# An LSTM layer with a residual: another order of the hidden units, row-wise weight copies, and x and the output moved in runs of 128 bytes

## The chip, the cores and the metric

The kernel runs on one core of a Trainium2 chip. The metric is the device time of one execution in microseconds. Before the change it was 2294.73 us (median of 3 runs, 2294.44 to 2298.69).

## The reference

x has shape (16, 512, 512): 16 sequences of 512 time steps with 512 features. `h0` (called `cond_1024`) is (16, 512), `Wx` and `Wh` are (512, 2048), `b` is (2048). All are float32.

```python
xW = einsum('ntd,dg->ntg', x, Wx) + b
def step((prev_h, prev_c), xw_t):
    a = xw_t + prev_h @ Wh
    i, f, o = sigmoid(a[:, :512]), sigmoid(a[:, 512:1024]), sigmoid(a[:, 1024:1536])
    g = tanh(a[:, 1536:])
    next_c = f * prev_c + i * g
    next_h = o * tanh(next_c)
return x + (next_h of all 512 steps)
```

The 512 steps depend on each other; `xW` does not depend on them, and can be computed ahead of the step that needs it.

## The kernel before

**Units and partitions.** There are 128 partitions, cut into four blocks of 32 (`NJ` = 4, index j). Each block takes 128 of the 512 hidden units or input features. With feature = 128j + 32c + u, partition block j holds the features 128j to 128j+127, of which the 32 x 32 transposes of VectorE bring feature u of chunk c to partition 32j + u. The rows of `Wx` and `Wh` have to lie in the same order: chunk c of partition 32j + u is row 128j + 32c + u. `load_w` (L124) copies a weight in transfers that each fill 32 partitions, two chunks at a time; its copies of `Wh` are issued by SP and ACT (4 each, L341), those of `Wx` by SP and POOL (8 each, L359).

**Steps and stages.** A stage is 8 time steps (`XB`), so there are 64 stages. Two steps form a pair, since 16 sequences fill half of a 32-row block; a stage has 4 pairs (`XP`). `load_xs` (L141) loads the x of one stage into a tile `xs` of 128 x 4 x 128: for each of the 4 feature blocks and each of the 2 steps of a pair it issues one DMA on SP's queue, of 16 partitions x 4 pairs x 512 bytes. That is 8 DMAs per stage. Stage s+2 is loaded in the first step of stage s (L519); `xs` has four buffers (L77).

**A step on the engines.** The program's order on each engine is written out by hand: `STEP_PE` and `STEP` name the operations of one step, and the loop from L485 emits them. TensorE runs `products` (L182, matmul at L188): the hidden state, in three float16 parts, times three float16 parts of `Wh` (`wq`), 96 matmuls of 256 columns per step, in groups of four that write the four 32-row blocks of a bank. Then `project` (L163, matmul at L165) computes `xW` of a later pair: 16 float32 matmuls of 512 columns per step. VectorE and ScalarE turn the gates into the next hidden state. In odd steps `turn_x` (L158) transposes the x of a later pair, of pair (t+5)/2 in step t, so the first pair of stage s is turned in step 8s-5. In even steps `residual` (L320) transposes the finished pair on VectorE and adds x on POOL into a tile `ob` (two buffers, L79).

**Output.** After the fourth pair of a stage `put` (L311) writes the whole `ob` with 8 DMAs on SP's queue, of 16 partitions x 4 pairs x 512 bytes. For the last two pairs it is called earlier, so that little is left at the end. In SP's queue the put of stage s-1 stands directly ahead of the load of stage s+2.

**DMA semaphores.** The DMAs of the SP and ACT queues go round over eight semaphores, and each DMA waits until the one that used its semaphore last has landed. At most eight are under way.

**The start.** Before step 0 the kernel finds the largest magnitude of each half of `Wh` (`bound`, L394), derives scales, splits `Wh` into its three float16 parts (`split`, L426) in 8 rounds n, turns x and h0 (L469, in round 3), projects the first two pairs (round 4), seeds the gate banks (`seed`, L174), and then runs step 0 with `first_products` (L197). The bias arrives by 8 broadcast DMAs on POOL's queue.

Of the kernel before, what the change touches and what calls it, by code (L numbers as in the profile page):

```python
# [7 lines left out]
FP = mybir.dt.float32  # L8
HP = mybir.dt.float16
I32 = mybir.dt.int32  # L10
AF = mybir.ActivationFunctionType
ALU = mybir.AluOpType
# [3 lines left out]
Q = 32  # L16
# [13 lines left out]

@with_exitstack
def lstm_residual(ctx: ExitStack, tc: tile.TileContext, x, h0, wx, wh, b, out):

# [61 lines left out]
    wh_sb = const.tile([P, NK, G * H], FP, tag="wh", name="wh_sb")  # L97
    wq = [const.tile([P, NK, G * H], HP, tag=f"wq{i}", name=f"wq{i}") for i in range(3)]

    wx_j = wx_sb.rearrange("p c (g j w) -> p c j g w", g=G, j=NJ)  # L100
    wh_j = wh_sb.rearrange("p c (e g j h u) -> p c e h j g u", e=2, g=2, j=NJ, h=2)
    wq_j = [w.rearrange("p c (g j h u) -> p c h j g u", g=G, j=NJ, h=2) for w in wq]
    bias = const.tile([P, G * P], FP, tag="bias", name="bias")
    mask = const.tile([P, S2], FP, tag="mask", name="mask")
    zero = const.tile([1, G * P], HP, tag="zero", name="zero")
    amax = const.tile([P, NK], FP, tag="amax", name="amax")
    top = const.tile([P, 2], FP, tag="top", name="top")
    bits = const.tile([P, 2, 2], FP, tag="bits", name="bits")
    sc = const.tile([P, 2, 4], FP, tag="sc", name="sc")
# [11 lines left out]
    ]  # L121
    xb = [psum.tile([P, G * P], FP, tag=f"xb{i}", name=f"xb{i}") for i in range(NXB)]

    def load_w(dst, w, c0, dmas, parts=1):  # L124


        n = G * H // parts
        for j in range(2):
            for q, dma in enumerate(dmas):
                r = w[(2 * q + j) * P + c0 * Q :][: 2 * Q].rearrange("(c u) f -> u c f", u=Q)  # L130
                p = slice((2 * q + j) * Q, (2 * q + j + 1) * Q)
                for e in range(parts):
                    a = parts - 1 - e
                    dma.dma_start(  # L134
                        out=dst[p, c0 : c0 + 2, a * n : (a + 1) * n],
                        in_=r[:, :, e * n : (e + 1) * n],
                    )

    xs = {}

    def load_xs(s, dma=nc.sync):  # L141

        xs[s] = xsp.tile([P, XP, P], FP, tag="xs", name=f"xs_{s}")
        for j in range(NJ):
            for r in range(S2):
                p0 = j * Q + r * N
                dma.dma_start(
                    out=xs[s][p0 : p0 + N],
                    in_=x[:, s * XB + r : (s + 1) * XB : S2, j * P : (j + 1) * P],
                )  # L150


    xT = {}
# [3 lines left out]

    def turn_x(q):  # L158
        s, i = divmod(q, XP)
        xT[q] = xtp.tile([P, NK, Q], FP, tag="xT", name=f"xT_{q}")  # L160
        nc.vector.transpose(xT[q].rearrange("p c m -> p (c m)"), xs[s][:, i])

    def project(q, c):  # L163
        for j in range(NJ):
            nc.tensor.matmul(  # L165
                xb[q % NXB][j * Q : (j + 1) * Q],
                lhsT=xT[q][:, c],
                rhs=wx_j[:, c, j],
                start=False,
                stop=(c == NK - 1),  # L170
                skip_group_check=True,
            )

# [135 lines left out]
        nc.scalar.mul(hs[p][:, a], hist[p // XP][:, p % XP, a], RSL[h])  # L309

    def put(s, i0, i1, dmas):  # L311
        for j in range(NJ):
            for r in range(S2):
                p0 = j * Q + r * N
                dmas[r % len(dmas)].dma_start(
                    out=out[:, s * XB + S2 * i0 + r : s * XB + S2 * i1 : S2, j * P : (j + 1) * P],
                    in_=ob[s][p0 : p0 + N, i0:i1],
                )

    def residual(p):  # L320
        s, i = divmod(p, XP)
        if i == 0:
            ob[s] = outp.tile([P, XP, P], FP, tag="ob", name=f"ob_{s}")
        hb = work.tile([P, P], FP, tag="hb", name=f"hb_{p}")
        nc.vector.transpose(hb, hs[p].rearrange("p c m -> p (c m)"))  # L325
        nc.gpsimd.tensor_tensor(ob[s][:, i], hb, xs[s][:, i], ALU.add)  # L326
        if p == NP - 1:
            put(s, i, i + 1, [nc.sync, nc.scalar])
        elif p == NP - 2:
            put(s, 0, i + 1, [nc.sync])  # L330
        elif i == XP - 1:
            put(s, 0, XP, [nc.sync])


    h_in = work.tile([P, P], FP, tag="h_in", name="h_in", bufs=1)
# [1 line left out]
    warm = const.tile([1, 1], FP, tag="warm", name="warm")  # L337
    brow = const.tile([1, G * H], FP, tag="brow", name="brow")
    ones = const.tile([1, Q], FP, tag="ones", name="ones")
    for c in (0, 2):  # L340
        load_w(wh_sb, wh, c, (nc.sync, nc.scalar))  # L341
    load_xs(0)
    nc.vector.memset(zero, 0.0)
    nc.vector.memset(h_in, 0.0)
    nc.vector.memset(ones, 1.0)
    for j in range(NJ):
        nc.sync.dma_start(out=h_in[j * Q : j * Q + N], in_=h0[:, j * P : (j + 1) * P])
    nc.gpsimd.dma_start(out=brow, in_=b.rearrange("(o f) -> o f", o=1))
    b_j = b.rearrange("(o e g j w) -> j e o g w", o=1, e=2, g=2, j=NJ)
    for j in range(NJ):  # L350
        for e in range(2):
            nc.gpsimd.dma_start(
                out=bias[j * Q : (j + 1) * Q, (1 - e) * GU : (2 - e) * GU].rearrange(
                    "p (g w) -> p g w", g=2
                ),
                in_=b_j[j, e].broadcast_to([Q, 2, P]),
            )
    for c in (0, 2):
        load_w(wx_sb, wx, c, (nc.sync, nc.gpsimd), 2)  # L359
    load_xs(1)  # L360

    for h in range(2):
# [14 lines left out]

    for bank in gates[0] + gates[1] + xb[3:]:  # L380
        zeros(bank, True)
    for bank in xb[:3]:
        for e in range(2):
            for j in range(NJ):
                nc.tensor.matmul(
                    bank[j * Q : (j + 1) * Q, (1 - e) * GU : (2 - e) * GU],
                    lhsT=ones,
                    rhs=brow.rearrange("p (e g j w) -> p e j g w", e=2, g=2, j=NJ)[:, e, j],
                    start=(e == 0),
                    stop=False,  # L390
                    skip_group_check=True,
                )

    def bound(c):  # L394
        if c == 1:
            junk = tmp.tile([P, G * H], HP, tag="junk", name="junk", bufs=1)
            nc.scalar.activation(junk, wh_sb[:, c], AF.Abs, accum_out=amax[:, c : c + 1])
        else:
            nc.vector.tensor_reduce(
                amax[:, c : c + 1],  # L400
                wh_sb[:, c],
                mybir.AxisListType.X,
                ALU.max,
                apply_absolute_value=True,
            )

    def scales(h):


        nc.vector.tensor_tensor(  # L410
            top[:, h : h + 1], amax[:, 2 * h : 2 * h + 1], amax[:, 2 * h + 1 : 2 * h + 2], ALU.max
        )
        t = top[:, h : h + 1].bitcast(I32)
        e, inv = bits[:, h, 0:1], bits[:, h, 1:2]
        nc.vector.tensor_scalar(
            inv.bitcast(I32), t, EXP, EXP, ALU.bitwise_and, ALU.bitwise_xor
        )
        nc.vector.tensor_scalar(e.bitcast(I32), t, EXP, None, ALU.bitwise_and)
        nc.vector.tensor_scalar(RS2[h], inv, 2.0**12, 0.5, ALU.mult, ALU.min)
        nc.vector.tensor_scalar(RS[h], inv, 2.0**13, 1.0, ALU.mult, ALU.min)  # L420
        nc.vector.tensor_scalar(S[h], e, 2.0**-14, 1.0, ALU.mult, ALU.max)
        nc.vector.tensor_scalar(RSL[h], RS[h], 1.0 / LO, None, ALU.mult)
# [3 lines left out]
    def split(n, k):  # L426

        c, e = divmod(n, 2)
        w = wh_sb[:, c, e * GH : (e + 1) * GH]
        f = [q[:, c, (1 - e) * GH : (2 - e) * GH] for q in wq]  # L430
        if k == 0:
            nc.scalar.mul(f[0], w, RS2[c // 2])
        elif k == 1:
            r1[n] = tmp.tile([P, GH], FP, tag="r1", name=f"r1_{n}")
            nc.vector.scalar_tensor_tensor(
                r1[n], w, RS[c // 2], f[0], ALU.mult, ALU.subtract
            )
        elif k == 2:
            nc.scalar.copy(f[1], r1[n])
        elif k == 3:  # L440
            r2[n] = tmp.tile([P, GH], FP, tag="r2", name=f"r2_{n}")
            nc.vector.tensor_tensor(r2[n], r1[n], f[1], ALU.subtract)
        else:
            nc.scalar.mul(f[2], r2[n], LO)

    NH = 2 * NK
    bound(0)
    bound(1)
    scales(0)
    split(0, 0)  # L450
    split(0, 1)
    split(1, 0)
    for n in range(NH):
        if n == 0:
            bound(2)
        if n == 2:
            bound(3)
            scales(1)
        if n + 1 < NH:
            split(n + 1, 1)  # L460
# [6 lines left out]
        if n == 3:  # L467
            for q in range(3):
                turn_x(q)  # L469
            nc.vector.transpose(hT0.rearrange("p c m -> p (c m)"), h_in)  # L470
        if n == 4:
            for c in range(NK):
                for q in range(2):
                    project(q, c)

            for _ in range(16):
                zeros(xb[3], False)
        if n == 6:
            for h in range(2):
                seed(0, h)  # L480
    split(NH - 1, 4)
    for h in range(2):
        seed(1, h)

    for t in range(T):  # L485
        s, ti = divmod(t, XB)
# [22 lines left out]
            if q + 1 < NP:  # L509
                turn_x(q + 1)  # L510
        else:
            if q + 1 < NP:
                put_bias(q + 1)
            if t:
                residual(t // 2 - 1)
# [33 lines left out]
```

## Time and profile before

| what | value |
|---|---|
| median of 3 runs | 2294.73 us |
| the profiled execution: time / span | 2294.09 us / 2291.7 us |
| granted clock of TensorE | 0.999 |
| PE busy | 2249.4 us, 98% |
| DVE, ACT, POOL busy | 1952.7 us (85%), 1838.1 us (80%), 127.2 us (6%) |
| SP: DMAs issued for x and for the output | 512 and 516 |
| first matmul of step 0 | 50.87 us after the start |

The span runs from the first to the last instruction. Busy time does not count instructions that issue DMAs, so SP has no row in the page's first part; its issues are seen in the timeline of its queue, where each piece has a start, a length and a count. In the list of waits a line says who waited for whom, how long in total and how often.

### The profile page before, as it was taken

The page shows a single profiled execution, that of the slowest core. Times are in us where ns is not written, and L with a number is a line of the kernel's source. Part 1 is how long each engine was busy: PE and PEld are TensorE (multiplying, and loading weights), DVE is VectorE, ACT ScalarE, POOL GpSimd, SP SyncE. Part 2 cuts the span into 40 slices and gives each one's busy share as a digit, 9 for nine tenths or more (in the row PEclk, how much of TensorE's full clock was granted, in tenths as well). Part 3 has the DMA queues.
Part 4 walks back from the last instruction along what each step waited for, and adds up shares of the span by engine and source line. Part 5 has one row for each costly group of instructions (what it writes and reads, how often), then busy time and mean ns, then how long its engine had stood idle before and what let it go on. Part 6 is the DMA issues. An engine that isn't in the chain of part 4 may idle for free.

```text
span 2291.7 us, 137735 instructions
## 1 busy us (share of the span) xinstructions
PE 2249.4 (98%) x57445; PEld 1572.7 (69%) x57445; DVE 1952.7 (85%) x11813; ACT 1838.1 (80%) x7959; POOL 127.2 (6%) x281
## 2 busy tenths in 40 slices
PE   4999999999999999999999999999999999999997
PEld 2677766777766777777666777776677777666775
DVE  5888888888888888888888888888888888888887
ACT  5888888888888888888888888888888888888887
POOL 1000000000000000000000000000000000000000
PEclk9999999999999999999999999999999999999999
DMA  7000000100100001000001001010000010010000
GB/s 166 13 21 15 22 18 17 22 15 20 22 14 22 22 13 22 21 14 22 17 18 22 15 20 22 13 22 22 13 22 19 17 22 18 17 22 15 20 18 12
DMA packets 85005, 51.10 MB, mean 22 GB/s; under 512 B 17104, under 2 KB 82720, under 8 KB 83872
## 3 DMA queue, kind: packets, MB, share of 16 engines
q1 hardware_dynamic: 83008, 37.82, 7.6%
q8 instruction: 452, 7.41, 1.4%
q0 software_dynamic: 928, 2.37, 0.5%
q10 hardware_dynamic: 448, 2.13, 0.4%
q14 instruction: 169, 1.38, 0.2%
HBM read 25.47 MB, written 16.78 MB: 18 GB/s over the span
## 4 chain that ended last, share of the span: by engine, by line
PE 98%; DMA 2%; DVE 0%; issue 0%; ACTq 0%; POOLq 0%; POOL 0%; SPq 0%
PE gates L188 59%; PE xb L165 38%; DMA wh_sb<-in_L_cond_Wh_dram 1%; DMA xs<-in_x_dram 0%; DMA wx_sb<-in_L_cond_Wx_dram 0%; PE gates L201 0%; PE xb L374 0%; ACTq L134 0%; DVE gt L224 0%; DVE preo L231 0%; DVE pre L231 0%; DVE parts L284 0%; DVE gto L224 0%; POOLq L544 0%; POOL ob L326 0%
## 5 line engine op out<-in xcount | busy, mean ns | idle before, releaser
L188 PEld LDWEIGHTS <-parts 128*32 128x32 f16 x49056 | 1307.1, 96 | 368.8 <-DVE parts L284 298.8
L188 PE MATMUL gates<-wq,parts 128*32 128x256 f16 x49056 | 1449.2, 273 | 4.2 <-DVE parts L284 4.2
L165 PE MATMUL xb<-wx_sb,xT 128*32 128x512 f32 x8192 | 977.1, 593 | 22.5 <-DMA wx_sb<-in_L_cond_Wx_dram 22.5
L224 DVE STREAM_TRANSPOSE gt<-gates 128x192 f32<-128x192 f32 x1024 | 391.7, 383 | 229.9 <-PE gates L188 170.7
L165 PEld LDWEIGHTS xb<-wx_sb,xT 128*32 128x32 f32 x8192 | 264.6, 110 | 327.5 <-issue 303.5
L258 ACT ACTIVATE gc<-pre 128x32 f32<-128x32 f32 x1022 | 234.7, 230 | 274.7 <-DVE pre L231 261.9
L175 ACT ACTIVATE gates<-xb,mask 128x256 f32<-128x256 f32 x1024 | 450.3, 440 | 2.1 <-PE xb L165 2.1
L266 ACT ACTIVATE os<-so,sc 128x32 f32<-128x32 f32 x1024 | 329.1, 321 | 16.6
L288 ACT COPY parts<-parts 128x32 f16<-128x32 f16 x1022 | 214.4, 210 | 131.7 <-DVE parts L284 131.7
L231 DVE SCALAR_TENSOR_TENSOR pre<-gt 128x96 f32<-128x96 f32 x1024 | 253.6, 248 | 0.0
L260 ACT ACTIVATE sif<-pre 128x64 f32<-128x64 f32 x1024 | 245.7, 240 | 0.0
L326 POOL TENSOR_TENSOR ob<-hb,xs 128x128 f32<-128x128 f32 x256 | 117.1, 457 | 2146.0 <-DVE hb L325 1732.5
L224 DVE STREAM_TRANSPOSE gto<-gates 128x64 f32<-128x64 f32 x1024 | 229.6, 224 | 0.0
L276 ACT ACTIVATE tch<-gc 128x32 f32<-128x32 f32 x1024 | 226.8, 221 | 0.3
L298 DVE SCALAR_TENSOR_TENSOR parts<-rem,parts 128x32 f16<-128x32 f32 x1022 | 196.3, 192 | 35.5
L264 ACT ACTIVATE so<-preo 128x32 f32<-128x32 f32 x1024 | 226.4, 221 | 0.0
L231 DVE SCALAR_TENSOR_TENSOR preo<-gto 128x32 f32<-128x32 f32 x1024 | 192.6, 188 | 17.5
L290 DVE SCALAR_TENSOR_TENSOR parts<-parts,hist 128x32 f16<-128x32 f16 x1022 | 192.0, 188 | 17.7
L268 DVE TENSOR_TENSOR pr<-sif,gc 128x64 f32<-128x64 f32 x1022 | 204.2, 200 | 0.0
L284 DVE TENSOR_TENSOR parts<-os,tch 128x32 f16<-128x32 f32 x1022 | 196.5, 192 | 0.0
L274 DVE TENSOR_TENSOR gc<-pr 128x32 f32<-128x32 f32 x1024 | 192.1, 188 | 0.0
L278 DVE SCALAR_TENSOR_TENSOR hist<-os,tch 128x32 f32<-128x32 f32 x1024 | 188.7, 184 | 0.3 <-ACT tch L276 0.3
(47 smaller groups left out, 730.8 us busy)
## 6 DMA issues: line engine op xcount, KB each, us to landing
xs<-in_x_dram SPq DMA_DIRECT2D x512, 32.0 KB, 2.0
out_dram<-ob SPq DMA_DIRECT2D x504, 32.0 KB, 1.7
wh_sb<-in_L_cond_Wh_dram ACTq DMA_DIRECT2D x4, 512.0 KB, 13.4
wh_sb<-in_L_cond_Wh_dram SPq DMA_DIRECT2D x4, 512.0 KB, 13.1
wx_sb<-in_L_cond_Wx_dram POOLq DMA_DIRECT2D x8, 256.0 KB, 9.5
wx_sb<-in_L_cond_Wx_dram SPq DMA_DIRECT2D x8, 256.0 KB, 6.8
bias<-in_L_cond_b_dram POOLq DMA_DIRECT2D x8, 32.0 KB, 13.4
out_dram<-ob SPq DMA_DIRECT2D x8, 24.0 KB, 1.6
```

Of the source, the lines that this page charges most:

```text
L165: nc.tensor.matmul(xb[q % NXB][j * Q : (j + 1) * Q], lhsT=xT[q][:, c], rhs=wx_j[:, c, j], start=False, stop=(c == NK - 1), skip_group_chec ...
L175: nc.scalar.mul(gates[h][t % 2][:, :GU].rearrange("p (g u) -> p g u", g=G), xb[t // 2 % NXB].rearrange("p (g h u) -> p h g u", g=G, h=2)[: ...
L188: nc.tensor.matmul(g[j * Q : (j + 1) * Q, :GU], lhsT=a[:, cc, k * N : (k + 2) * N], rhs=wq_j[i - 1][:, 2 * kh + cc, h, j], start=False, st ...
L224: nc.vector.transpose(gt.rearrange("p b m -> p (b m)"), gates[h][t % 2][:, b0 * Q : b1 * Q])
L231: nc.vector.scalar_tensor_tensor(pre.rearrange("p g (c n) -> p (g c) n", c=2), gt[:, :, (1 - t % 2) * N : (2 - t % 2) * N], 1.0 / LO, gt[: ...
L258: nc.scalar.activation(gc[h][:, 0], v["pre", h][:, 0], AF.Tanh)
L260: nc.scalar.activation(new("sif", t, h, [P, 2, 2 * N]), v["pre", h][:, 1:3], AF.Sigmoid)
L264: nc.scalar.activation(new("so", t, h, [P, 2 * N]), v["preo", h][:, 0], AF.Sigmoid)
L266: nc.scalar.mul(new("os", t, h, [P, 2 * N]), v["so", h], S[h])
L268: nc.vector.tensor_tensor(new("pr", t, h, [P, 2, 2 * N]), v["sif", h], gc[h], ALU.mult)
L276: nc.scalar.activation(new("tch", t, h, [P, 2 * N]), gc[h][:, 1], AF.Tanh)
L288: nc.scalar.copy(slots(t, h, 2), slots(t, h, 0))
```

## The change

**Other order of the units.** Feature 128c + 32j + u now lies on partition 32j + u of chunk c, for the inputs, the hidden state and the gates. Chunk c of a weight is then 128 consecutive rows, one for each partition. Each weight is copied by 8 DMAs of 128 partitions x 1024 columns (4 KB rows), all on SP's queue; ACT and POOL no longer copy weights. Block j of x and of the output is now four runs of 32 floats (128 bytes) for each time step, 128 floats apart, in place of one run of 512 bytes.

**x and output.** A DMA [...] covers one time step: `load_xs` issues 32 DMAs of 8 KB per stage, in place of 8 of 32 KB. `put` likewise, and it is called for each pair (8 DMAs of 8 KB) in place of each stage. The x of stage 0 goes over POOL's queue. Ahead of the first transpose of a stage VectorE copies one column of each pair into a small tile `seen`, which waits for all DMAs of the stage at once.

**Matmul operands.** The column order of the gates in PSUM is g, c, u. The moving operands are views of the weights: `wq` in runs of 32 float16 (64 bytes, before 128), `wx_sb` in runs of 32 float32 (128 bytes, before 512).

**Start.** The bias no longer comes by 8 DMAs; ScalarE copies it once from a bank that TensorE has filled. `brow` is loaded over ACT's queue. The bound of the last chunk of `Wh` is shared between ScalarE and VectorE, two of the eight last parts of the split go to VectorE, the projections come one round earlier, 12 in place of 16 filling matmuls with zeros follow them (into a gate bank), and the seeds of both first steps come together.

```diff
-    wx_j = wx_sb.rearrange("p c (g j w) -> p c j g w", g=G, j=NJ)
-    wq_j = [w.rearrange("p c (g j h u) -> p c h j g u", g=G, j=NJ, h=2) for w in wq]
+    wx_j = wx_sb.rearrange("p k (g c j u) -> p k j g c u", g=G, c=NK, j=NJ)
+    wq_j = [
+        w.rearrange("p k (g h c j u) -> p k h j g c u", g=G, h=2, c=2, j=NJ) for w in wq
+    ]
...
+    x_j = x.rearrange("n t (c j u) -> j n t c u", c=NK, j=NJ)
+    out_j = out.rearrange("n t (c j u) -> j n t c u", c=NK, j=NJ)
...
     def load_xs(s, dma=nc.sync):
         xs[s] = xsp.tile([P, XP, P], FP, tag="xs", name=f"xs_{s}")
-        for j in range(NJ):
-            for r in range(S2):
-                p0 = j * Q + r * N
-                dma.dma_start(
-                    out=xs[s][p0 : p0 + N],
-                    in_=x[:, s * XB + r : (s + 1) * XB : S2, j * P : (j + 1) * P],
-                )
+        for i in range(XP):
+            for j in range(NJ):
+                for r in range(S2):
+                    p0 = j * Q + r * N
+                    dma.dma_start(
+                        out=xs[s][p0 : p0 + N, i].rearrange("p (c u) -> p c u", c=NK),
+                        in_=x_j[j, :, s * XB + i * S2 + r],
+                    )
...
     def turn_x(q):
         s, i = divmod(q, XP)
+        if i == 0:
+            seen = tmp.tile([P, XP], FP, tag="seen", name=f"seen_{s}")
+            nc.vector.tensor_copy(seen, xs[s][:, :, 0])
...
     def put(s, i0, i1, dmas):
-        for j in range(NJ):
-            for r in range(S2):
-                p0 = j * Q + r * N
-                dmas[r % len(dmas)].dma_start(
-                    out=out[:, s * XB + S2 * i0 + r : s * XB + S2 * i1 : S2, j * P : (j + 1) * P],
-                    in_=ob[s][p0 : p0 + N, i0:i1],
-                )
+        for i in range(i0, i1):
+            for j in range(NJ):
+                for r in range(S2):
+                    p0 = j * Q + r * N
+                    dmas[r % len(dmas)].dma_start(
+                        out=out_j[j, :, s * XB + S2 * i + r],
+                        in_=ob[s][p0 : p0 + N, i].rearrange("p (c u) -> p c u", c=NK),
+                    )
...
         if p == NP - 1:
             put(s, i, i + 1, [nc.sync, nc.scalar])
-        elif p == NP - 2:
-            put(s, 0, i + 1, [nc.sync])
-        elif i == XP - 1:
-            put(s, 0, XP, [nc.sync])
+        else:
+            put(s, i, i + 1, [nc.sync])
...
-    for c in (0, 2):
-        load_w(wh_sb, wh, c, (nc.sync, nc.scalar))
-    load_xs(0)
+    nc.scalar.dma_start(out=brow, in_=b.rearrange("(o f) -> o f", o=1))
+    for c in range(NK):
+        for e in range(2):
+            f = slice(e * GH, (e + 1) * GH)
+            nc.sync.dma_start(out=wh_sb[:, c, f], in_=wh[c * P : (c + 1) * P, f])
+    load_xs(0, nc.gpsimd)
...
-    for c in (0, 2):
-        load_w(wx_sb, wx, c, (nc.sync, nc.gpsimd), 2)
+    for c in range(NK):
+        for e in range(2):
+            nc.sync.dma_start(
+                out=wx_sb[:, c, (1 - e) * GH : (2 - e) * GH],
+                in_=wx[c * P : (c + 1) * P, e * GH : (e + 1) * GH],
+            )
     load_xs(1)
```

More of the change, by code (lines that the diff above doesn't have):

```diff
@@ L98, in lstm_residual @@
     wq = [const.tile([P, NK, G * H], HP, tag=f"wq{i}", name=f"wq{i}") for i in range(3)]
-    wx_j = wx_sb.rearrange("p c (g j w) -> p c j g w", g=G, j=NJ)
-    wh_j = wh_sb.rearrange("p c (e g j h u) -> p c e h j g u", e=2, g=2, j=NJ, h=2)
-    wq_j = [w.rearrange("p c (g j h u) -> p c h j g u", g=G, j=NJ, h=2) for w in wq]
+    wx_j = wx_sb.rearrange("p k (g c j u) -> p k j g c u", g=G, c=NK, j=NJ)
+    wh_j = wh_sb.rearrange(
+        "p k (e g h c j u) -> p k e h j g c u", e=2, g=2, h=2, c=2, j=NJ
+    )
+    wq_j = [
+        w.rearrange("p k (g h c j u) -> p k h j g c u", g=G, h=2, c=2, j=NJ) for w in wq
+    ]
     bias = const.tile([P, G * P], FP, tag="bias", name="bias")
@@ L105, in lstm_residual @@
     zero = const.tile([1, G * P], HP, tag="zero", name="zero")
-    amax = const.tile([P, NK], FP, tag="amax", name="amax")
+    amax = const.tile([P, NK + 1], FP, tag="amax", name="amax")
     top = const.tile([P, 2], FP, tag="top", name="top")
@@ L122, in lstm_residual @@
     xb = [psum.tile([P, G * P], FP, tag=f"xb{i}", name=f"xb{i}") for i in range(NXB)]
[L124 to L133, printed above, removed]
-                    dma.dma_start(
-                        out=dst[p, c0 : c0 + 2, a * n : (a + 1) * n],
-                        in_=r[:, :, e * n : (e + 1) * n],
-                    )
+    x_j = x.rearrange("n t (c j u) -> j n t c u", c=NK, j=NJ)
+    out_j = out.rearrange("n t (c j u) -> j n t c u", c=NK, j=NJ)
+    h0_j = h0.rearrange("n (c j u) -> j n c u", c=NK, j=NJ)
     xs = {}
@@ L143, in load_xs @@
         xs[s] = xsp.tile([P, XP, P], FP, tag="xs", name=f"xs_{s}")
-        for j in range(NJ):
-            for r in range(S2):
-                p0 = j * Q + r * N
-                dma.dma_start(
-                    out=xs[s][p0 : p0 + N],
-                    in_=x[:, s * XB + r : (s + 1) * XB : S2, j * P : (j + 1) * P],
-                )
+        for i in range(XP):
[6 more added lines that the diff above has]
+                    )
     xT = {}
@@ L169, in project @@
                 start=False,
-                stop=(c == NK - 1),
+                stop=False,
                 skip_group_check=True,
@@ L311, in put @@
     def put(s, i0, i1, dmas):
-        for j in range(NJ):
-            for r in range(S2):
-                p0 = j * Q + r * N
-                dmas[r % len(dmas)].dma_start(
-                    out=out[:, s * XB + S2 * i0 + r : s * XB + S2 * i1 : S2, j * P : (j + 1) * P],
-                    in_=ob[s][p0 : p0 + N, i0:i1],
-                )
+        for i in range(i0, i1):
[6 more added lines that the diff above has]
+                    )
     def residual(p):
@@ L345, in lstm_residual @@
     nc.vector.memset(ones, 1.0)
+    load_xs(0, nc.gpsimd)
     for j in range(NJ):
[L347 to L350, printed above, removed]
+        nc.sync.dma_start(
+            out=h_in[j * Q : j * Q + N].rearrange("p (c u) -> p c u", c=NK), in_=h0_j[j]
+        )
+    for c in range(NK):
         for e in range(2):
[L352 to L356, printed above, removed]
-            )
-    for c in (0, 2):
-        load_w(wx_sb, wx, c, (nc.sync, nc.gpsimd), 2)
+            nc.sync.dma_start(
+                out=wx_sb[:, c, (1 - e) * GH : (2 - e) * GH],
+                in_=wx[c * P : (c + 1) * P, e * GH : (e + 1) * GH],
+            )
     load_xs(1)
@@ L376, in zeros @@
         )
-    for bank in gates[0] + gates[1] + xb[3:]:
+    for bank in gates[0] + gates[1]:
         zeros(bank, True)
-    for bank in xb[:3]:
+    for bank in xb:
         for e in range(2):
@@ L387, in lstm_residual @@
                     lhsT=ones,
-                    rhs=brow.rearrange("p (e g j w) -> p e j g w", e=2, g=2, j=NJ)[:, e, j],
+                    rhs=brow.rearrange("p (e g c j u) -> p e j g c u", e=2, g=2, c=NK, j=NJ)[
+                        :, e, j
+                    ],
                     start=(e == 0),
@@ L392, in lstm_residual, with bound @@
                 )
[L394 to L397, printed above, removed]
+    nc.scalar.copy(bias, xb[0])
+    def bound(i, c, on_act, f=slice(0, G * H)):
+        w = wh_sb[:, c, f]
+        if on_act:
+            junk = tmp.tile([P, G * H], HP, tag="junk", name=f"junk_{i}", bufs=1)
+            nc.scalar.activation(junk[:, f], w, AF.Abs, accum_out=amax[:, i : i + 1])
         else:
             nc.vector.tensor_reduce(
-                amax[:, c : c + 1],
-                wh_sb[:, c],
+                amax[:, i : i + 1],
+                w,
                 mybir.AxisListType.X,
@@ L407, in scales @@
     def scales(h):
-        nc.vector.tensor_tensor(
-            top[:, h : h + 1], amax[:, 2 * h : 2 * h + 1], amax[:, 2 * h + 1 : 2 * h + 2], ALU.max
+        nc.vector.tensor_reduce(
+            top[:, h : h + 1], amax[:, 2 * h : 2 + 3 * h], mybir.AxisListType.X, ALU.max
         )
@@ L442, in split @@
             nc.vector.tensor_tensor(r2[n], r1[n], f[1], ALU.subtract)
+        elif n in (3, 7):
+            nc.vector.tensor_scalar(f[2], r2[n], LO, None, ALU.mult)
         else:
@@ L446, in lstm_residual @@
     NH = 2 * NK
-    bound(0)
-    bound(1)
+    bound(0, 0, False)
+    bound(1, 1, True)
     scales(0)
@@ L453, in lstm_residual @@
     for n in range(NH):
-        if n == 0:
-            bound(2)
+        if n == 1:
+            bound(2, 2, False)
         if n == 2:
-            bound(3)
+            bound(3, 3, True, slice(0, GH))
+            bound(4, 3, False, slice(GH, 2 * GH))
             scales(1)
@@ L470, in lstm_residual @@
             nc.vector.transpose(hT0.rearrange("p c m -> p (c m)"), h_in)
-        if n == 4:
             for c in range(NK):
@@ L474, in lstm_residual @@
                     project(q, c)
[L476 to L480, printed above, removed]
+            for _ in range(12):
+                zeros(gates[0][1], False)
+        if n == 5:
+            for t in range(2):
+                for h in range(2):
+                    seed(t, h)
     split(NH - 1, 4)
-    for h in range(2):
-        seed(1, h)
     for t in range(T):
@@ L511, in lstm_residual @@
         else:
-            if q + 1 < NP:
+            if t and q + 1 < NP:
                 put_bias(q + 1)
```

## The prediction

> **What bounds the kernel now.** I read the page's busy times and its chain first, then the chain in order of time, then SP's queue, which no busy row shows.
>
> ```profile
> PE 98%; DMA 2%; DVE 0%; issue 0%; ACTq 0%; POOLq 0%; POOL 0%; SPq 0%
> ...
> L188 PE MATMUL gates<-wq,parts 128*32 128x256 f16 x49056 | 1449.2, 273 | 4.2 <-DVE parts L284 4.2
> L165 PE MATMUL xb<-wx_sb,xT 128*32 128x512 f32 x8192 | 977.1, 593 | 22.5 <-DMA wx_sb<-in_L_cond_Wx_dram 22.5
> ```
>
> TensorE is on the path from 38 us to the end and almost never waits. In order of time the chain is:
>
> ```profile
> 38.05 9.27 PE xb L165 x64
> 47.31 3.56 PE xb L374 x16
> 50.87 3.63 PE gates L201 x128
> 54.50 1.72 PE xb L165 x16
> 56.22 2.80 PE gates L188 x96
> 59.02 1.72 PE xb L165 x16
> 60.73 2.64 PE gates L188 x96
> ```
>
> Step 0 begins at 50.87 us, and every step after it costs 1.72 + 2.64 = 4.36 us. So 512 steps take 2232.3 us, and 2291.7 - 50.9 - 2232.3 = 8.5 us are the tail. A stage of 8 steps is 34.9 us.
>
> SP's queue (start, length, issues), two groups of eight:
>
> ```profile
> 232.91 3.71 SPq L315 DMA_DIRECT2D out_dram<-ob  x8
> 236.71 4.81 SPq L147 DMA_DIRECT2D xs<-in_x_dram  x8
> ```
>
> SP issues 16 DMAs per stage, for about 9 of 34.9 us. Both groups have eight equal DMAs, yet the second takes 1.1 us more. The DMA view of exactly that second stretch says what else ran:
>
> ```profile
> q1 hardware_dynamic: 612, 0.25, 21.2%
> q8 instruction: 1, 0.02, 1.5%
> q14 instruction: 1, 0.01, 0.6%
> ```
>
> The first stretch has a packet of queue 14 but none of queue 8. Queue 8 carries instructions in packets of 16 KB, 452 of them in the span; they are mostly TensorE's program (224 instructions a step by the page's counts, 64 bytes each on average: 14 KB a step). I matched the trace's single records. After 100 us SP has 65 groups of issues, 972 DMAs in 558.0 us, 0.574 us each. An undisturbed issue takes 0.424 us and the next starts 0.045 us later: a pitch of 0.469. It does not depend on the DMA: 16 runs of 512 bytes took 0.418, 64 runs of 8 KB 0.420. 106 packets of queue 8 began inside these groups, and **each of the 106** met an issue longer than 0.7 us; the excess over 0.424 averaged 0.99 us. The 8 KB packets of queue 14 alone cost next to nothing: 6 of 44 met a stall of their own, 0.06 us on the mean of 44.
>
> **SP's queue after the change.** A stage has 32 DMAs of x and 4 x 8 of the output, 64 on one queue in place of 16.
> - Issue: 64 x 0.469 = 30.0 us. A DMA is again 64 runs on 16 partitions; only the run is 128 bytes, and the issue time did not follow the run's length between 512 bytes and 8 KB.
> - Fetches: 423 packets of queue 8 between 100 and 2192 us are 7.06 a stage. When SP issues all the time, all of them meet an issue: 7.06 x 0.99 = 7.0 us.
> - Small terms: five second waits a stage (a put waits for POOL and for its semaphore) at 0.05 us, and queue 14, 0.18: 0.4 us.
> - Sum: **37.4 us of SP a stage, against 34.9 us of TensorE.** SP becomes the bound.
>
> Here a rule decides: the Trainium skill, "Runtime: NRT & Kernel Launch", section "Instruction fetch mechanics", says that crossing a 16 KiB block of instructions costs one step of a DMA queue, mostly hidden. For the engine that fetches, the trace agrees (PE waits 4.2 us in all at L188). By that rule a stage is 30.0 + 0.4 = 30.4 us, SP keeps up, and the time moves by the start alone. The row is about another engine, SP, and 106 of 106 decide for 37.4.
>
> **When it bites.** SP's order in a stage is put of the last pair, load of stage s+2, then three puts. The load of a stage is due after step 8s-5, where `seen` holds VectorE; all of the stage behind it waits. It is first issued in step 8(s-2), 11 steps or 48 us ahead, and needs 32 x 0.58 + 2.0 (landing) = 21 us. The spare of about 27 us is used up at 2.5 us a stage after some 11 stages; from there SP's sum sets the time. Puts are late too, but `ob` has two buffers, nearly two stages of room. The end follows from SP's work alone. It is continuous from the put of pair 3, at T0 + 8 x 4.36 + 4.3, to the load of stage 63: 61 loads (1952 DMAs) and 241 puts (1928), 3880 DMAs or 60.6 x 64, 60.6 x 37.4 = 2268 us, plus 2.0 to land. That x is awaited at the end of step 499; about 2 us of TensorE's next products overlap the wait. 12 steps (52.3 us) and the tail (8.5) follow. The last puts, without loads beside them, fit in.
>
> **The start, T0.** ACT and POOL lose 4 and 8 weight copies, SP issues 16 DMAs of 512 KB instead of 4 + 8. Eight megabytes of weights landed by 37.9 us at about 240 GB/s; with 4 KB rows on all partitions I keep 35 to 38. What is late next is the x of stage 0: 32 DMAs on POOL's queue, each waiting for the eighth before it. POOL's row is the bias before: its copies landed at 12.3, 13.9, 16.2, 17.8, 19.8, 21.8 us, 1.9 us apart under weight traffic, while POOL issues one in 0.53. If the first lands near 10 and they follow so until 35 us, 14 have landed; the other 18 at 0.53 and a landing of 2 make 46. VectorE stands at `seen` until then. One microsecond of transposes, 9.27 of projection, 12 x 0.22 of zeros: T0 = 59. If weight traffic doesn't slow them, they land by 32 x 0.53 + 2 = 19 us, Wx binds, and T0 = 35 + 9.3 + 2.7 = 47; in the best case, weights at the 328 GB/s that the skill's "SBUF — State Buffer" (Door 1) gives for 128 partitions, 8.4 MB are an estimated 26 us, and T0 = 40. I take 57, near the row. The shared bound and the two parts moved to VectorE (about 1 us each) lie beside these waits; the dropped bias DMAs free POOL for the x above. Without the cover each is 1 us of the start.
>
> **The sum.** 57 + 34.9 + 4.3 = 96; + 2268 + 2 = 2366; - 2 + 52.3 + 8.5 = 2425 us of span; the profiled run lay 2.4 us over its span, and 0.6 us below the median: **2428 us**, slower by 5.8%.
>
> **Edits costed at nothing.** `seen` is one small VectorE copy a stage (0.1 us of 34.9, VectorE is 85% busy); its wait is the one above. The put per pair moves no work of POOL. Runs of 64 bytes in `wq` and 128 in `wx_sb`: TensorE reads 256 columns in 2.64 / 24 = 110 ns with runs of 128 bytes, and a project group of 512 in 430 ns with runs of 512 bytes[...]: no run shows a price. Each 1 ns per added run would be 4 x 24 + 12 x 4 to 8 = 0.14 to 0.19 us a step; up to (37.4 - 34.9) / 8 = 0.31 it hides behind SP. It can't gain.
>
> **Packets.** x and output make four times as many. "DMA: Bandwidth & Descriptors" (Specifications) wants 512 bytes for full rate and has shorter ones read, modified and written. The row: 1120 packets took 22.6% of 16 engines in 9.5 us, 31 ns each. 64 DMAs x 70 packets x 31 ns / 16 = 8.7 us a stage; twice that is 17. By row or rule, no bound.
>
> **Rivals.**
> 1. *SP keeps up, and only the start moves, to the faster side.* It decides if a fetch costs a busy SP under (34.9 - 30.4) / 7.06 = 0.63 us. For it: stalls that could shrink with 8 KB DMAs, which leave the engines sooner. Against: 0.99, and the whole range of run lengths. Time 2294.7 + (T0 - 50.9): 2284 at T0 = 40, 2303 at 59. Faster needs T0 below 46.3. Chance 0.12.
> 2. *The limit of eight under way.* If 128-byte runs land later than 8 x 0.469 = 3.75 us (now 2.0 for x, 1.7 for out, 3.9 at most), the pitch is landing / 8. At 5 us it is 0.625, a stage 40 us plus part of the fetches: 2600 to 2800. Chance 0.05.
> 3. *TensorE reads short runs more slowly.* Beyond 0.31 us a step TensorE is the bound again: 2294 + 512 x 0.4 = 2500 at 0.4. Chance 0.05.
>
> The forecast keeps 0.78.
>
> **How the numbers follow.** In the forecast itself the stage lies between 36.0 (0.8 us a fetch) and 39.2 (1.1 us, pitch 0.475): 60.6 x 1.4 = 85 us less, 60.6 x 1.8 = 109 more: 2343 to 2537. With the start, 2335 to 2545; below lies most of rival 1, above most of rival 2, about 0.17 together. A measurement can tell 0.2% (4.6 us) from no change. Rival 1 splits into faster 0.05, same 0.03, slower 0.04; the rest is slower: 0.92.
>
> **What would show it.** SP's timeline without gaps from about 100 us; eight issues in 4.6 to 4.7 us on average; a wait of VectorE's `seen` for the x DMAs, about 2 us a stage after the first ten stages, 130 us in total, TensorE idle as long; steps elsewhere still 4.36 us; POOL's waits for DMA small. Wrong it would be if SP waits for POOL in every stage (rival 1), if x lands after 4 us (2), or if L188 and L165 take longer with no wait (3).

## The result, and the profile after

The changed kernel takes 2427.57 us (median of 5 runs, 2421.34 to 2434.24) against 2295.58 us before (5 runs): a ratio of 1.0577, 95% interval 1.0555 to 1.0599. The forecast was 2428. The profiled execution took 2433.03 us, with a span of 2431.1.

The page's chain of the changed kernel, shares of the span by engine and by line, and the two matmul groups:

```profile
PE 48%; SPq 37%; DVE 7%; issue 4%; DMA 4%; ACT 1%; DVEq 0%; POOLq 0%; POOL 0%
...
L188 PE MATMUL gates<-wq,parts 128*32 128x256 f16 x49056 | 1465.3, 274 | 9.0 <-DVE parts L284 6.6
L165 PE MATMUL xb<-wx_sb,xT 128*32 128x512 f32 x8192 | 995.1, 603 | 114.5 <-DVE xT L161 94.5
```

Before, the chain was TensorE to 98%. Now SP's queue holds 37% of it, and TensorE waits 114.5 us ahead of the projections, 94.5 us of it for the transposed x. In the chain in order of time a step is still 1.72 + 2.64 us where nothing waits:

```profile
66.64 1.72 PE xb L165 x16
68.35 2.64 PE gates L188 x96
70.99 1.72 PE xb L165 x16
```

The difference sits in a few steps. Of the 511 intervals between steps 66 are longer than 4.5 us, and together these late steps lose 147.2 us by the trace's records. Step 1, the first with the main products, starts 7.1 us earlier than before; 147.2 - 7.1 = 140.1 us, and the spans differ by 139.4.

Not all of the 147 us is waiting. In some late steps the matmuls are slower too: after the wait that ends at 984.2 us the granted clock is 0.50 from 985.5 to 988.9 us, and 1.00 in the 7 us ahead of 982 and behind 989. There are 15 such stretches of 3.4 or 6.8 us between 300 and 2250 us, and none before the change until 2288.5 us. TensorE is busy for 2298.6 us in place of 2249.4, and the mean of a projection matmul is 603 ns in place of 593; all stretches at half clock, 79 us, would lose an estimated 40 us. This adds nothing to the time here, since SP's queue sets the length of a stage and does not stop for it.

SP's queue in the changed kernel (start, length, issues) has no gap:

```profile
999.28 19.30 SPq L143 DMA_DIRECT2D xs<-in_x_dram  x32
1018.68 18.91 SPq L316 DMA_DIRECT2D out_dram<-ob  x32
1037.69 19.08 SPq L143 DMA_DIRECT2D xs<-in_x_dram  x32
1056.88 17.96 SPq L316 DMA_DIRECT2D out_dram<-ob  x32
```

Each group of 32 follows the one before it within about 0.1 us. From load to load it is 38.4 us here; the mean of 58 stages by the trace's records is 37.63, against 34.9 before. The list of waits names who pays (in total, times, longest):

```profile
DVE seen L159 <- DMA out_dram<-ob: 143.0, 59, 5.9
...
PE xb L165 <- DVE xT L161: 94.5, 42, 4.9
```

`seen` waits for x, but the line names the DMA of an output. Loads and puts share eight semaphores, and the list names the semaphore update that came last before `seen` ran. The records of the last load show what it waited for: SP ends its last issue of x at 2372.53 us, this DMA has landed at 2373.90, and `seen` runs at 2374.28. The put that the list names was issued after that load, on another semaphore, and landed at 2374.06. On average the wait is 143.0 / 59 = 2.4 us a stage.

### The profile page after: what moved, and what is told of

It reads as the page before. It is cut to its first block, busy times and chain, and to the rows that moved or that the text cites. A ratio compares the mean times of both kernels' runs of the same rounds, so it can differ in the third digit from the quotient of the medians.

```text
span 2431.1 us, 141071 instructions
## 1 busy us (share of the span) xinstructions
PE 2298.6 (95%) x57456; PEld 1570.6 (65%) x57456; DVE 1952.3 (80%) x11879; ACT 1838.0 (76%) x7959; POOL 134.2 (6%) x296
## 3 DMA queue, kind: packets, MB, share of 16 engines
q0 software_dynamic: 1024, 0.26, 0.1%
## 4 chain that ended last, share of the span: by engine, by line
PE 48%; SPq 37%; DVE 7%; issue 4%; DMA 4%; ACT 1%; DVEq 0%; POOLq 0%; POOL 0%
SPq L143 34%; PE gates L188 30%; PE xb L165 18%; DMA out_dram<-ob 3%; SPq L316 2%; DVE gt L224 1%; DVE pre L231 1%; DVE gto L224 1%; DVE pr L268 1%; DVE preo L231 1%; DVE parts L284 1%; DMA xs<-in_x_dram 0%; DVE gc L274 0%; DMA wh_sb<-in_L_cond_Wh_dram 0%; DVE xT L161 0%
## 5 line engine op out<-in xcount | busy, mean ns | idle before, releaser
L188 PE MATMUL gates<-wq,parts 128*32 128x256 f16 x49056 | 1465.3, 274 | 9.0 <-DVE parts L284 6.6
L165 PE MATMUL xb<-wx_sb,xT 128*32 128x512 f32 x8192 | 995.1, 603 | 114.5 <-DVE xT L161 94.5
```

The lines of the kernel that those rows point to most:

```text
L165: nc.tensor.matmul(xb[q % NXB][j * Q : (j + 1) * Q], lhsT=xT[q][:, c], rhs=wx_j[:, c, j], start=False, stop=False, skip_group_check=True,)
L188: nc.tensor.matmul(g[j * Q : (j + 1) * Q, :GU], lhsT=a[:, cc, k * N : (k + 2) * N], rhs=wq_j[i - 1][:, 2 * kh + cc, h, j], start=False, st ...
```

## The experiments

Four questions were open: whether the number of DMAs on SP is the cause or something else in the change; whether SP's queue is a threshold or each DMA costs something; whether the stalls at instruction fetches (the 16 KB packets of queue 8) are part of SP's sum; and whether TensorE's shorter runs hide a loss of their own. Ratios are to the kernel before, timed again beside each group of runs.

### Only the split, with runs of 512 bytes

The kernel before, in `load_xs` and in `residual`:

```diff
-        for j in range(NJ):
-            for r in range(S2):
-                p0 = j * Q + r * N
-                dma.dma_start(
-                    out=xs[s][p0 : p0 + N],
-                    in_=x[:, s * XB + r : (s + 1) * XB : S2, j * P : (j + 1) * P],
-                )
+        for i in range(XP):
+            for j in range(NJ):
+                for r in range(S2):
+                    p0 = j * Q + r * N
+                    dma.dma_start(
+                        out=xs[s][p0 : p0 + N, i],
+                        in_=x[:, s * XB + i * S2 + r, j * P : (j + 1) * P],
+                    )
...
-        elif p == NP - 2:
-            put(s, 0, i + 1, [nc.sync])
-        elif i == XP - 1:
-            put(s, 0, XP, [nc.sync])
+        else:
+            put(s, i, i + 1, [nc.sync])
```

> The kernel before with one thing changed: x is loaded by 32 DMAs of 8 KB a stage in place of 8 of 32 KB, and the output is put pair by pair, also 32 DMAs of 8 KB a stage. Runs stay 512 bytes, units, weights and start stay as before. If the number of DMAs on SP's queue is the cause, a stage of SP is 64 x 0.469 + 7 fetches x 1.0 + 0.5 = 37.5 us as in the changed kernel, and the time is near 2435 us (2415 to 2455; its start is some 7 us later than the changed kernel's). If the runs of 128 bytes, or the operands' short runs, are the cause, it stays at 2295.

Measured: 2408.06 us, ratio 1.0493 (1.0473 to 1.0513). SP's queue:

```profile
1003.18 18.87 SPq L148 DMA_DIRECT2D xs<-in_x_dram  x32
1022.15 19.13 SPq L316 DMA_DIRECT2D out_dram<-ob  x32
1041.38 18.09 SPq L148 DMA_DIRECT2D xs<-in_x_dram  x32
```

Layout, run length and operands are those of the kernel before, and most of the loss is there: the number of DMAs makes it. The time is 7 us under the expected range. Against the changed kernel two terms are smaller. The stage is 37.1 us in place of 37.63, some 30 us in all: the usual issue took 0.418 us here and 0.424 in the changed kernel, and a stall was 0.02 us shorter. The kernel lacks `seen`, so each transpose waits for its own pair; from the last x issue to the end are 51.5 us in place of 58.6. One term is larger: SP issues without a gap from 102.6 us on, in the changed kernel from 87.8, mostly because the x of stage 0 stands in SP's queue with 32 DMAs ahead of `Wx`. The expectation had both starts only 7 us apart.

### 48 DMAs a stage

The same, but the output is put every second pair:

```diff
-        else:
-            put(s, i, i + 1, [nc.sync])
+        elif p == NP - 2:
+            put(s, i, i + 1, [nc.sync])
+        elif i % 2:
+            put(s, i - 1, i + 1, [nc.sync])
```

> As the split kernel with runs of 512 bytes, but the output is put every two pairs: 16 DMAs a stage, so SP has 48 a stage. If SP's queue is a bound with a threshold, 48 x 0.469 + 7 x 1.0 + 0.4 = 30 us fits under TensorE's 34.9 us and the time stays at 2295 (within 6 us). If each DMA costs the path something of its own (contention with TensorE's instruction fetches, or engines that wait), two thirds of the 48 added DMAs give two thirds of the loss: about 2385.

Measured: 2305.01 us, ratio 1.0035 (1.0021 to 1.0049). By the records the stage is 34.91 us, that of TensorE, and of the 511 intervals between steps only five are over 4.5 us, with 0.8 us lost in all. So there is a threshold, and 32 more DMAs a stage than before cost TensorE's steps nothing as long as SP stays below it. The 9 us are the start again: the first hidden state is written at 66.6 us, 10.5 later than before. The expectation of "within 6 us" had left out that start and was missed. SP has room here:

```profile
1000.75 16.41 SPq L316 DMA_DIRECT2D out_dram<-ob  x16
1017.26 19.45 SPq L148 DMA_DIRECT2D xs<-in_x_dram  x32
```

The 16 puts spread over 16.41 us because the second eight wait for POOL.

### 96 DMAs a stage

The split kernel, with each load of x also cut in two halves of 64 features:

```diff
-                    dma.dma_start(
-                        out=xs[s][p0 : p0 + N, i],
-                        in_=x[:, s * XB + i * S2 + r, j * P : (j + 1) * P],
-                    )
+                    for f in range(2):
+                        dma.dma_start(
+                            out=xs[s][p0 : p0 + N, i, f * 64 : (f + 1) * 64],
+                            in_=x[:, s * XB + i * S2 + r, j * P + f * 64 : j * P + (f + 1) * 64],
+                        )
```

> The kernel before with x by 64 DMAs of 4 KB a stage (runs of 256 bytes) and the output by 32 of 8 KB: 96 a stage. A SP-bound stage by the sum: 96 x 0.465 = 44.6, fetches 7.06 x 1.0, small terms 0.6: 52.3 us. SP is without a gap from about 45 us on; 63 loads of x and 241 puts are 5960 DMAs or 62.1 times 96, 3247 us; with 57 us of last steps about 3350 us (3280 to 3430). If issue gets cheaper when the queue never empties, or if only the loads' waits count, it is under 3200.

Measured: 3353.41 us (2 runs), ratio 1.4594 (1.4565 to 1.4623). The stage is 51.7 us.

```profile
1037.26 33.47 SPq L149 DMA_DIRECT2D xs<-in_x_dram  x64
1070.83 17.98 SPq L317 DMA_DIRECT2D out_dram<-ob  x32
```

Far over the threshold the same sum still gives the time: 52.3 us a stage were expected. The usual issue is no cheaper with DMAs of 4 KB and a queue that never empties (0.417 us on the mean, 0.419 before). The late steps now lose about 16 us a stage and the granted clock of TensorE averages 0.867, but the stage is still what SP's sum makes it.

### Fewer instruction fetches

The changed kernel without the four product groups of the second weight part (a third of all products, so it does not compute the LSTM):

```diff
-STEP_PE = "q3aa q3ab q1ab q1aa q2aa q3ba q1ba q2ba q2bb q1bb q2ab q3bb x0 x1"
+STEP_PE = "q3aa q3ab q2aa q3ba q2ba q2bb q2ab q3bb x0 x1"
```

> The changed kernel without a third of the products (the four groups of the second weight part are left out, so the result is not the LSTM's): 160 TensorE instructions a step in place of 224, 10 KB, so 5.0 instruction fetches a stage in place of 7. SP's 64 DMAs are the same. If each fetch stalls SP by 1.0 us, a stage goes from 37.65 to 37.65 - 2.0 = 35.65 us and the time to about 2305 us (2285 to 2325). If SP is bound by its own issue time or by the landing of its DMAs alone, a stage stays at 37.65 and the time at 2428.

Measured: 2306.54 us, ratio 1.0042 (1.0021 to 1.0063). SP's 64 DMAs are untouched, and it is still the bound:

```profile
1020.05 17.83 SPq L143 DMA_DIRECT2D xs<-in_x_dram  x32
1037.98 17.43 SPq L316 DMA_DIRECT2D out_dram<-ob  x32
1055.51 17.77 SPq L143 DMA_DIRECT2D xs<-in_x_dram  x32
```

The DMA view between 100 and 2192 us counts the instruction packets, first of the changed kernel, then of this one:

```profile
q8 instruction: 396, 6.49, 1.3%
```

```profile
q8 instruction: 301, 4.93, 1.0%
```

The stage fell from 37.63 to 35.58 us, by 2.05, with about two fetches less in it. In the records, 415 issues between 150 and 2250 us took over 0.7 us in the changed kernel, by 0.99 us more than 0.424; here it is 316 in the same stretch, again by 0.99, and the other issues are as long as there (0.422 us). That the stalls come with TensorE's fetches and count in full once SP is the bound is shown. SP is the bound by about 1 us only: a step without a wait takes 4.32 us here, 34.5 us a stage, so still fewer fetches would have gained little.

### x over POOL's queue

The changed kernel, with the x of stage s+2 issued by POOL, 8 DMAs in each even step:

```diff
-    def load_xs(s, dma=nc.sync):
-        xs[s] = xsp.tile([P, XP, P], FP, tag="xs", name=f"xs_{s}")
-        for i in range(XP):
+    def load_xs(s, dma=nc.sync, i0=0, i1=XP):
+        if i0 == 0:
+            xs[s] = xsp.tile([P, XP, P], FP, tag="xs", name=f"xs_{s}")
+        for i in range(i0, i1):
...
-        if ti == 0 and s + 2 < NS:
-            load_xs(s + 2)
+        if ti % 2 == 0 and s + 2 < NS:
+            load_xs(s + 2, nc.gpsimd, ti // 2, ti // 2 + 1)
```

> The changed kernel with the x of stage s+2 issued by POOL, 8 DMAs in each even step, in place of SP. SP keeps 32 DMAs a stage, 15 us plus fetches. If SP's issue is the bound, the whole loss goes: TensorE's 34.9 us a stage are back, and with the changed kernel's earlier start (step 0 at 41.2 in place of 50.9, of which step 1 keeps 7) about 2288 us, 0.3% under the kernel before. If TensorE reads the shorter runs more slowly or 128-byte packets clog the DMA engines, it stays over 2400. If POOL's descriptor writing is held up by VectorE, POOL's adds come late and the time lies between, 2300 to 2400.

Measured: 2291.19 us, ratio 0.9977 (0.9967 to 0.9986): the whole loss is gone, and the kernel is 0.2% faster than the kernel before. Of 511 intervals between steps nine are over 4.5 us, with 1.5 us lost. The chain is TensorE's again:

```profile
PE 97%; DMA 1%; issue 1%; DVE 0%; POOL 0%; ACT 0%; POOLq 0%
```

Runs of 64 and 128 bytes in the operands and 128-byte packets are all in this kernel, and a step takes 4.36 us as before, so neither costs TensorE anything that is seen here. The instructions that load x on POOL (shortest, median, longest in ns):

```profile
L144 POOL DMA_DIRECT2D xs<-in_x_dram x2016: 512/512/646, 1.3 to 2211.6; - x184
```

POOL's issue is longer than SP's, but even, and each of POOL's adds still starts within 0.09 us of its transpose, so POOL is not held up. By the records 251 packets of queue 8 met an issue of POOL, and those issues took 0.512 us on the mean, like all others. The stall is seen on SP's issues and not on POOL's; ACT's queue was not tried. Between this kernel and the expected 2288 lie 3 us.

### Without the wait for a whole stage

```diff
-        if i == 0:
-            seen = tmp.tile([P, XP], FP, tag="seen", name=f"seen_{s}")
-            nc.vector.tensor_copy(seen, xs[s][:, :, 0])
```

> The changed kernel without the copy into seen: each transpose waits for the DMAs of its own pair, not for the whole stage. The load of a stage is then due 24 DMAs or 14 us later for its first pair. If SP's sum is the bound, a stage stays at 37.6 us, the first late step comes some 5 stages later, and the time falls by about 14 us to 2414 (2405 to 2420). If the whole-stage wait itself makes the loss, it falls to near 2295.

Measured: 2421.68 us, ratio 1.0534 (1.0517 to 1.0552); its interval ends just below that of the changed kernel, so the gain is small, and the time is just above the expected range (2405 to 2420). The stage is 37.61 us, as expected. The first step that is late by over 1 us is 107 in place of 75, four stages later, and the late steps sum to 125.8 us in place of 147.2. That should have brought some 20 us; the spans of the profiled executions differ by 8. The rest is in SP's queue at the end, first of the changed kernel, then of this one:

```profile
2372.64 55.93 SPq L316 DMA_DIRECT2D out_dram<-ob  x92
```

```profile
2368.94 52.00 SPq L312 DMA_DIRECT2D out_dram<-ob  x92
```

92 DMAs of the output are left after the last load. In the changed kernel SP still waits 3.9 us for the last pair; in this one the last hidden state is written at 2408.6 us and SP issues without such a wait until 2420.9. Its backlog of puts now sets the end. The backlog also reaches POOL: by the records the first add of a stage starts up to 4.6 us late in 37 stages, behind the last put of its `ob` buffer; in the changed kernel no add is late. So VectorE's wait for the whole stage was the first thing to give way, and SP's sum is the floor below it.

## Why the prediction was right

**SP's stage: right, and by its terms.** Predicted 37.4 us, measured 37.63. In the records between 150 and 2250 us (55.8 stages) the undisturbed issues take 0.422 and the gaps 0.049: 64 x 0.471 = 30.1, where 30.0 stood. Stalls: 415 / 55.8 x 0.99 = 7.4, where 7.0 and the share of queue 14 in 0.4 stood. The rest, 0.2, is 30 longer gaps. Of 427 fetches that began inside SP's groups after 150 us every one met a stalled issue, as the 106 did before.

One bound of the stage was summed wrongly: a pitch of 0.475 and 1.1 us a fetch make 30.4 + 7.8 + 0.4 = 38.6 us, not 39.2, so the upper end of the range should have been about 2500 and not 2537. The forecast itself doesn't use it.

**The rule against the row: the row held.** Fetches that are hidden from the engine that fetches are not hidden from SP; the kernel with fewer fetches shows what they are worth.

**The start: wrong, by 16 us to the slow side at step 0 and by 13 at step 1.** The step that failed is the row taken for POOL's x: the bias copies before, which landed 13.4 us after their issue. The x on the same queue took 5.5.

```profile
bias<-in_L_cond_b_dram POOLq DMA_DIRECT2D x8, 32.0 KB, 13.4
```

```profile
xs<-in_x_dram POOLq DMA_DIRECT2D x32, 8.0 KB, 5.5
```

POOL had issued all 32 by 24.5 us, and `seen` ran at 29.4 us, where 46 stood. TensorE in the changed kernel:

```profile
29.90 8.67 PE L165 MATMUL xb<-wx_sb,xT 128*32 128x512 f32 x64 [19.85 <-DMA xs<-in_x_dram]
38.50 2.76 PE L372 MATMUL gates<-zero 1*128 1x512 f16 x12
41.19 3.70 PE L201 MATMUL gates<-wh_sb,hT 128*32 128x128 f32 x128
44.71 1.90 PE L165 MATMUL xb<-wx_sb,xT 128*32 128x512 f32 x16
49.10 4.28 PE L188 MATMUL gates<-wq,parts 128*32 128x256 f16 x96 [2.49 <-DVE parts L284]
```

Step 0 begins at 41.19 and not at 57. Step 1 begins at 49.10, after 2.49 us of waiting: VectorE takes up the gates of step 0 only at 46.86 us, behind the last pieces of the split, one of which waits 6.3 us for ScalarE. The prediction had all of the split covered by the waits for x. Before, step 1 began at 56.22; the start is 7 us faster, where 6 us slower were predicted. The weights were faster as well: in its first 30 us the core moved 293 GB/s, before 216 in the first 40. By the records the 8.4 MB of both weights moved between 1.7 and 27.3 us, which is 328 GB/s, the 128-partition figure of the Trainium skill's "SBUF — State Buffer" (Door 1); before, they took until 42.0 us, and 37.9 is only when the projections could begin. The prediction's best case built on that figure, T0 = 40, was nearer than its old row.

**The end.** SP was continuous from 88 us, predicted 96. From there to the last x issue at 2372.5 it took 2284.5 us, predicted 2268 (the same 3880 DMAs); the rest of the span was 58.6, predicted 61. The errors are -8, +16 and -2: a start too late and a stage too short by 0.23 us nearly cancel. That the forecast fits the median within 1 us is partly luck; the span of the profiled execution is 6 us above the 2425 of the sum.

**The onset** came at step 75, after nine stages (0.5 us were lost at step 67); 11 were predicted.

**The signs.** `seen` waited 143.0 us in all, where 130 stood. TensorE stood idle for x only 94.5 us of it, not as long: the rest of the late steps is in part its slower clock, which the prediction did not have. POOL's waits for DMA were small as predicted, though the list of waits puts 462.9 us down to x: by the records each of the 256 adds starts 0.08 us after its transpose on VectorE has ended.

**The rivals.** *SP keeps up*: it would have needed stalls under 0.63 us, they were 0.99; its best side is seen in the kernel with x on POOL, which has the start without the queue. *Eight under way*: DMAs of 8 KB landed earlier, not later, after 1.8 us for x and 1.5 for the output:

```profile
out_dram<-ob SPq DMA_DIRECT2D x2044, 8.0 KB, 1.5
xs<-in_x_dram SPq DMA_DIRECT2D x2016, 8.0 KB, 1.8
```

Before:

```profile
xs<-in_x_dram SPq DMA_DIRECT2D x512, 32.0 KB, 2.0
out_dram<-ob SPq DMA_DIRECT2D x504, 32.0 KB, 1.7
```

*Short runs*: no price, by the kernel with x on POOL. The prediction's own comparison could not show it, since its 110 ns are of float16 matmuls and its 430 ns of float32.

**The packets** were costed too high, without effect: x and output took 10.1% of the DMA engines, where 8.7 of 37.4 us (23%) stood.

```profile
q1 hardware_dynamic: 284339, 29.34, 10.1%
```

A packet of 128 bytes took 12.6 ns on the mean, not 31. One of 512 bytes took 35 ns before and 30 in the kernel with only the split, so a quarter of the bytes takes more than a third of the time. Whether part of that is the read, modify and write that the Trainium skill's "DMA: Bandwidth & Descriptors" (Specifications) has for packets under 512 bytes can't be told from these times.

## What to carry to other kernels

A queue that issues DMAs has a throughput of its own, though no busy row shows it: count its DMAs in the repeating stage, multiply by the pitch read from a group without a gap, add what stalls it, and compare with the stage of the engine that bounds. Here cutting transfers into smaller ones was free in the loop until that sum passed the stage (48 DMAs), and from there all of the excess was paid in every stage (64 and 96). When a layout needs more and smaller DMAs, give part of them to a queue that has time, and look at the order of the queue at the start as well as in the loop.

## What was not expected

SP's issue of a DMA stalls by about 0.99 us at practically every 16 KB instruction packet of another engine's program, in the kernels before and after (106 of 106, 427 of 427), while POOL's issue does not (251 packets met one; the issues they met took 0.512 us on the mean, as all others). Which part of the machine makes SP wait was not tried; the runs show only that the stalls come with the packets and fall with their number. The second surprise is the weight load: with rows over 128 partitions on one queue the core moved 293 GB/s in its first 30 us, with 32-partition copies on the queues of SP, ACT and POOL 216 in its first 40. Which of the differences makes it (partitions, row length, queues) was not tried.
